# Causal attention: three fixed band buffers, blocks 2 and 0 of the queries in turns, fewer exponential and partial-sum buffers

## The chip, the cores and the metric

The kernel runs on one NeuronCore of a Trainium2 chip. A core has five engines that run side by side, each working through its own queue in order: TensorE (PE in the profile) multiplies matrices into eight PSUM banks, VectorE (DVE) reduces and adds, ScalarE (ACT) evaluates functions such as exp, GpSimd (POOL) does general arithmetic on SBUF, and SyncE (SP) issues DMA transfers. The metric is the device time of one execution in microseconds. The kernel before takes 4444.89 us, the median of 3 runs (4442.46 to 4447.12).

## The reference, cut to what matters

The whole is a chain of six residual layers on x of shape (2, 2048, 256): a mixture of experts, full attention, again the mixture, a gated recurrence, causal attention with relative positions, and the recurrence again. Only the fifth is changed:

```python
q = rotary(shape(x @ w_q.T)) / sqrt(16);  k = rotary(shape(x @ w_k.T));  v = shape(x @ w_v.T)
scores = einsum('bhqd,bhkd->bhqk', q, k)
rel = rel_emb[clip(pos_k - pos_q, -32, 32) + 32]
scores = scores + einsum('bhqd,qkd->bhqk', q, rel)
attn = softmax(where(causal, scores, -1e18))
ctx = einsum('bhqk,bhkd->bhqd', attn, v) + einsum('bhqk,qkd->bhqd', attn, rel)
out = ctx @ w_o.T
```

There are 16 heads of size 16. Because of the mask only relative positions from -32 to 0 occur, and all keys more than 31 behind a query share one position vector. Only a band of 32 keys behind each query therefore needs its own position terms.

## The kernel before, in words

The causal stage is `attention1`. Each batch's 2048 queries are cut into four blocks of 512 (`qc` 0 to 3), and the heads into four sets of four (`g`). A *group* is (batch, block, head set); there are 32. Block qc attends to the key blocks 0 to qc, so its size is 2(qc+1) *steps* of two half-steps each.

For each group there are two phases. In the score phase (`largest`), TensorE multiplies queries by keys and VectorE takes each query's largest score. The key vector shared by all far keys is folded into the keys (`kbias`), so far pieces need only a row maximum (L970). Near pieces, 160 keys wide, also get their own position term and their mask: they are added to a *band* tile in SBUF and written back to it (L986). The band comes from DRAM: `by_position` multiplies the queries by the position vectors (L924), ScalarE copies the product (L929), SyncE stores it skewed (L931) and reads it back shifted by one element per row (L939), which lines position terms up with keys. When a quarter of the band is done, the negated maximum is formed (L996) and added to the band on POOL (L1000); when all are done, SyncE stores the band to DRAM (pd, L1008).

In the exponential phase, TensorE computes the transposed far scores again (L1047, L1040) and brings the bands in by transposes (L1057, L1061), ScalarE takes exp into pT tiles (L1068), and TensorE multiplies these by the values half a step later (L1076). ScalarE copies each product to a `part` tile (L558) and POOL adds it to the output (L560). The position part of the output is read from pd (s<-pd, L1085), exponentiated (L1093), transposed (L1098) and multiplied (L1104). `divide` (L569 to L573) and `outputs` end a group.

Queries and keys are made by `rotate`: a projection (L138), a copy (L888), a shuffle (L890), and three or four POOL operations (L891 to L895); its temporaries, the product of `by_position` and the position exponentials share four `s2` buffers. Layer norms for the next blocks run on POOL too (L113).

The order on TensorE, ScalarE and VectorE is written out by hand. A loop over the groups fills Ms, Me (first and last score step), Es, Ee (exponential steps) and Rs (position step). Everything else is put at a step relative to these, and a last loop walks through the steps, interleaving the exponentials of one group with the scores of the next, head by head. The order on SyncE and POOL is made by a scheduler from dependencies. The groups of blocks 1 and 0 alternate, then come the four of block 2 and the four of block 3. Band tiles come from a pool of two buffers, so the plan lets a score phase start only when the band of the group two before it is nearly used up:

```python
if n > 1:
    start = max(start, min(Ee[n - 2] + 1, Es[n - 2] + 5) + 2 - (size - 2))
if n > 3:
    start = max(start, Ee[n - 4] + 4)
```

pT tiles have 12 buffers, part tiles 4.

Of the kernel before, what the change touches and what calls it, by code (L numbers as in the profile page):

```python
# [10 lines left out]
F32 = mybir.dt.float32  # L11
# [6 lines left out]
P = 128  # L18
B = 2
S = 2048  # L20
D = 256
H = 16
DH = 16
NT = B * S
NC = NT // P
TB = 512
NTB = NT // TB
CPB = TB // P
SB = S // TB
# [3 lines left out]
G = 4  # L33
J = 4
BAND = 32
BW = P + BAND
# [6 lines left out]
def macaron_kernel(ctx: ExitStack, tc: tile.TileContext, t: dict, out: bass.AP):  # L43
    nc = tc.nc
# [437 lines left out]
    HV = H // 2  # L482
    VW = DH + 1

    class Pieces:
# [32 lines left out]
        def values(self, v, wv, b, qc, half, row):  # L518

            w = HV * VW  # L520
            nc.gpsimd.memset(v[:, :, w:], 0.0)
            dst = v[:, :, 0:w].rearrange("p k (h d) -> p k h d", d=VW)
            nc.gpsimd.memset(dst[:, :, :, DH:], 1.0)
            pv = bank()
            for c in range(CPB):
                for kc in range(2):
                    nc.tensor.matmul(  # L527
                        pv[:, ts(c, P)], lhsT=self.xnT(b, qc)[:, kc, ts(c, P)],
                        rhs=wv[:, kc, ts(half, P)], start=kc == 0, stop=kc == 1,
                    )  # L530
            pv = pv.rearrange("p (k h d) -> p k h d", k=CPB, h=HV)
            if row is None:
                nc.scalar.copy(dst[:, :, :, 0:DH], pv)
            else:
                nc.vector.tensor_tensor(
                    dst[:, :, :, 0:DH], pv,
                    row[:, ts(half, P)].rearrange("p (o h d) -> p o h d", o=1, h=HV)
                    .to_broadcast([P, CPB, HV, DH]), ALU.add,
                )

# [7 lines left out]
                )  # L548
            nc.vector.tensor_tensor(self.q[t], self.q[t], pm, ALU.add)  # L549

        def gather(self, t, pv, q0=0):

            if t not in self.o:
                self.o[t] = self.wk.tile([P, TB], F32, name="o")
                nc.scalar.copy(self.o[t], pv)
                return
            part = self.wk.tile([P, TB], F32, name="part", bufs=4)
            nc.scalar.copy(part[:, q0:], pv[:, q0:])  # L558
            o = self.o[t][:, q0:]
            nc.gpsimd.tensor_tensor(o, o, part[:, q0:], ALU.add)  # L560
# [39 lines left out]
    class Jobs(dict):  # L600
        def at(self, step, fn, *args):
            self.setdefault(step, []).append((fn, args))
# [6 lines left out]
    def attention0(norm, tail, wq, wk_, wv, wo, bff):  # L609
# [7 lines left out]
        with ExitStack() as s:  # L617
            z = Pieces(s, "a0", norm, wo, bff)
# [50 lines left out]
            def weighted(t, kb):  # L669
                b, qc, g = groups[t]  # L670
                pv = bank()
                for j in range(J):
                    h = (g % 2) * J + j
                    nc.tensor.matmul(  # L674
                        pv[rows(j), :], lhsT=v[b, g // 2][:, kb, ds(h * VW, 32)],
                        rhs=z.pTs.pop((t, kb, j)), start=True, stop=True,
                    )
                z.gather(t, pv)

            jobs = Jobs()  # L680
            at = jobs.at
# [179 lines left out]
    def attention1(norm, tail, w, relk, relv, kbias, dramp, skew):  # L861
# [4 lines left out]
        with ExitStack() as s:  # L866
# [1 line left out]
            wk, q = z.wk, z.q  # L868
            groups = []
            for b in range(B):  # L870
                groups += [(b, qc, g) for g in range(G) for qc in (1, 0)]
                groups += [(b, qc, g) for qc in range(2, SB) for g in range(G)]
            NG = len(groups)
            kT, v, mx, band, cos, sin, wb, wT, st, pd, lead = ({} for _ in range(11))
            MX = SB + 1

            def tables(b, qc):
                for d, n in ((cos, "cos"), (sin, "sin")):
# [37 lines left out]
            def by_position(t):  # L916

                b, qc, g = groups[t]
                pr = bank()
                for qb in range(CPB):
                    nc.tensor.matmul(  # L924
                        pr[:, ts(qb, P)], lhsT=q[t][:, ts(qb, P)], rhs=relk,
                        start=True, stop=True,
                    )
                u = wk.tile([P, CPB * J, BAND], F32, name="s2", bufs=4)
                nc.scalar.copy(u.rearrange("p a d -> p (a d)"), pr)  # L929
                flat = skew[t % len(skew)]  # L930
                nc.sync.dma_start(  # L931
                    out=flat.rearrange("s (r w) -> r s w", w=UW)[:, :, P : P + BAND], in_=u
                )
                lead[t] = wk.tile([P, P - BAND + CPB * J * BW], F32, name="band")
                nc.gpsimd.memset(lead[t][:, 0 : P - BAND], 0.0)
                c = band[t] = lead[t][:, P - BAND :].rearrange(
                    "p (a j k) -> p a j k", a=CPB, j=J
                )
                nc.sync.dma_start(  # L939
                    out=c.rearrange("p a j k -> p (a j) k"),  # L940
                    in_=flat[:, P - 1 : P - 1 + P * (UW - 1)].rearrange(
                        "s (r w) -> r s w", w=UW - 1
                    )[:, :, 0:BW],
                )
# [119 lines left out]

            def exp(t, kb, j):
                q0 = max(0, kb - groups[t][1] * CPB) * P
                z.pTs[t, kb, j] = wk.tile([P, TB], F32, name="pT", bufs=12)
                nc.scalar.activation(z.pTs[t, kb, j][:, q0:], st.pop((t, kb, j))[:, q0:], AF.Exp)  # L1068

            def weighted(t, kb):  # L1070
                b, qc, g = groups[t]
                q0 = max(0, kb - qc * CPB) * P
                pv = bank()
                for j in range(J):
                    h = (g % 2) * J + j
                    nc.tensor.matmul(  # L1076
                        pv[rows(j), q0:],
                        lhsT=v[b, kb // CPB, g // 2][:, kb % CPB, ds(h * VW, 32)],
                        rhs=z.pTs.pop((t, kb, j))[:, q0:], start=True, stop=True,
                    )  # L1080
                z.gather(t, pv, q0)

            def positions_load(t):
                wb[t] = wk.tile([P, CPB, J * BAND], F32, name="s2", bufs=4)
# [17 lines left out]
            def positions(t):  # L1102
                pv = bank()
                nc.tensor.matmul(pv, lhsT=relv, rhs=wT[t], start=True, stop=True)  # L1104
                z.gather(t, pv)


            Ms, Me, Es, Ee, Rs = [], [], [], [], []
            for n, (b, qc, g) in enumerate(groups):
                size = 2 * (qc + 1)  # L1110
                start = Me[-1] + 1 if n else 0
                if n > 1:
                    start = max(start, min(Ee[n - 2] + 1, Es[n - 2] + 5) + 2 - (size - 2))
                if n > 3:
                    start = max(start, Ee[n - 4] + 4)
                Ms.append(start)
                Me.append(start + size - 1)
                start = Me[-1] + 2
                if n:
                    start = max(start, Ee[-1] + 1)  # L1120
                Es.append(start)
                Ee.append(start + size - 1)
                Rs.append(start + (3 if size == 2 else 4))
# [6 lines left out]
            jobs = Jobs()  # L1130
            at = jobs.at
            index = {x_: n for n, x_ in enumerate(groups)}
            for b in range(B):
                for qc in range(SB):
                    f = min(Ms[index[b, 1 if qc == 0 else qc, 0]], Ms[index[b, qc, 0]])
                    at(f - 12, tables, b, qc)
                    if b or qc > 1:
                        at(f - 12, z.ln_stats, b, qc)
                        at(f - 7, z.ln_transpose, b, qc)
                    for g in range(G):  # L1140
                        f = Ms[index[b, max(qc, 1), g]]
                        at(f - 4 + (qc == 0), keys, b, qc, g)
                    for half in range(2):
                        at(Es[index[b, max(qc, 1), 2 * half]] - 1 + (qc == 0), vals, b, qc, half)
            for n, (b, qc, g) in enumerate(groups):
                early = max(Ms[n] - 6, Ee[n - 4] + 1) if n > 3 else Ms[n] - 6
                at(early, queries, n)
                at(min(early + 2, Ms[n]), by_position, n)
                at(Me[n] + 1, z.subtract, n)
                at(Rs[n] - 3, positions_load, n)  # L1150
                at(Rs[n] - 2, positions_exp, n)
                at(Rs[n] - 1, positions_T, n)
                at(Rs[n], positions, n)
                end = max(Rs[n], Ee[n] + 1)
                at(end + 1, z.divide, n, b, qc, g, False)
                if g == G - 1:
                    at(end + 2, z.outputs_T, b, qc)
                    at(end + 3, z.outputs, b, qc, 0)
                    at(end + 4, z.outputs, b, qc, 1)
# [161 lines left out]
def _layout(i):  # L1321
# [47 lines left out]
        relv[d, a], relv0[d, a] = near, rel[0][None, :]  # L1369
        rel0[a, 0] = rel[0]  # L1370
    o["relk"], o["relk0"], o["relv"], o["relv0"], o["rel0_col"] = relk, relk0, relv, relv0, rel0
    o["a1_rel0_row"] = np.broadcast_to(np.tile(rel[0], H), (P, D))


    o["krow"] = np.zeros((P, 1), f)
# [29 lines left out]
```

## Time and profile before

| what | value |
|---|---|
| median of 3 runs | 4444.89 us (4442.46 to 4447.12) |
| profiled execution | 4446.38 us |
| its span, first to last instruction | 4444.6 us |
| mean granted TensorE clock | 0.969 |
| full attention stage, about | 440 to 2160 us |
| causal stage, first projection to last output | 2822 to 4259 us |
| instructions | 77325 |

The profile is of one execution. Times in its rows are microseconds from the span's start, durations of one instruction nanoseconds. PE is TensorE's multiplying, PEld its loading of weights. A matmul's end is modelled, so that TensorE's busy share overstates its work. A group is given by line, engine, operation and tiles (out<-in), then its count, busy time and mean, and the idle time of the engine before it with what ended that. A wait reads "who waited <- for what", with the total, the number and the longest. PEclk and the clock column are the share of full speed that TensorE was granted. A float32 matmul has two records, a transpose one.

### The profile page before, as it was taken

The page shows a single profiled execution, that of the slowest core. Times are in us where ns is not written, and L with a number is a line of the kernel's source. Part 1 is how long each engine was busy: PE and PEld are TensorE (multiplying, and loading weights), DVE is VectorE, ACT ScalarE, POOL GpSimd, SP SyncE. Part 2 cuts the span into 40 slices and gives each one's busy share as a digit, 9 for nine tenths or more (in the row PEclk, how much of TensorE's full clock was granted, in tenths as well). Part 3 has the DMA queues.
Part 4 walks back from the last instruction along what each step waited for, and adds up shares of the span by engine and source line. Part 5 has one row for each costly group of instructions (what it writes and reads, how often), then busy time and mean ns, then how long its engine had stood idle before and what let it go on. Part 6 is the DMA issues. An engine that isn't in the chain of part 4 may idle for free.

```text
span 4444.6 us, 77325 instructions
## 1 busy us (share of the span) xinstructions
PE 4178.2 (94%) x28512; PEld 2000.7 (45%) x28512; DVE 2711.3 (61%) x6176; ACT 2543.0 (57%) x5155; POOL 1825.1 (41%) x1694
## 2 busy tenths in 40 slices
PE   6798999999999999999968989799999999999999
PEld 3455433333343333333335545555544455554445
DVE  4234787887766778787442343455776645767633
ACT  2232488887877788888712322245566754566742
POOL 3226133335433333333350330366556576555520
PEclk8899999999999999999989999899999999999999
DMA  6242000000000000000232320254322344422201
GB/s 234 93 121 72 1 1 1 1 1 1 1 1 2 1 1 1 1 1 8 69 115 87 118 64 1 57 108 104 81 62 49 64 86 104 86 58 58 44 21 38
DMA packets 355514, 224.41 MB, mean 50 GB/s; under 512 B 146497, under 2 KB 338497, under 8 KB 355137
## 3 DMA queue, kind: packets, MB, share of 16 engines
q1 hardware_dynamic: 342848, 185.89, 16.7%
q0 software_dynamic: 12288, 33.57, 2.4%
q8 instruction: 227, 3.72, 0.4%
q14 instruction: 151, 1.23, 0.1%
HBM read 114.29 MB, written 105.12 MB: 49 GB/s over the span
## 4 chain that ended last, share of the span: by engine, by line
PE 82%; DVE 7%; POOL 3%; issue 3%; another core or an unknown queue 2%; DMA 2%; ACT 1%; SPq 0%; POOLq 0%; ACTq 0%; DVEq 0%
PE s L662 12%; PE s L674 11%; PE s L138 11%; PE s L650 10%; PE s L1076 5%; PE s L962 5%; PE s L358 5%; PE s L1047 5%; PE s L377 3%; PE s L592 1%; PE s L527 1%; PE s L1057 1%; PE s L1040 1%; PE s L1061 1%
## 5 line engine op out<-in xcount | busy, mean ns | idle before, releaser
L560 POOL TENSOR_TENSOR o<-o,part 128x512 f32<-128x512 f32 (+3 forms) x800 | 962.4, 1203 | 1418.9 <-ACT part L558 1414.6
L654 DVE TENSOR_REDUCE mx<-s 128x1 f32<-128x512 f32 x2048 | 1271.9, 684 | 365.4 <-PE s L650 364.4
L667 ACT ACTIVATE pT<-s 128x512 f32<-128x512 f32 x2048 | 1064.4, 618 | 207.3 <-PE s L650 202.4
L650 PE MATMUL s<-kT,q 32*128 32x512 f32 x4096 | 1016.6, 619 | 7.7 <-DVE mx L654 6.3
L662 PE MATMUL s<-q,kT 32*128 32x512 f32 x4096 | 1017.3, 617 | 6.3 <-DVE q L549 5.4
L1068 ACT ACTIVATE pT<-s 128x512 f32<-128x512 f32 (+3 forms) x1280 | 589.9, 546 | 269.6 <-PE s L1047 115.2
L662 PEld LDWEIGHTS s<-q,kT 32*128 32x128 f32 x4096 | 414.2, 184 | 472.2 <-DVE mx L654 310.5
L970 DVE TENSOR_REDUCE mx<-s 128x1 f32<-128x512 f32 (+1 forms) x768 | 472.0, 678 | 217.7 <-PE s L962 209.9
L558 ACT COPY part<-s 128x512 f32<-128x512 f32 (+3 forms) x800 | 466.6, 585 | 220.6 <-PE s L1076 101.9
L674 PE MATMUL s<-pT,v 128*32 128x512 f32 x4096 | 549.9, 605 | 2.0 <-DVE mx L654 1.9
L650 PEld LDWEIGHTS s<-kT,q 32*128 32x128 f32 x4096 | 405.4, 184 | 139.3 <-ACT pT L667 71.1
L358 PE MATMUL s<-we,xT 128*128 x592 | 289.1, 612 | 37.8 <-ACT xT L353 19.7
L962 PE MATMUL s<-kT,q 32*128 32x512 f32 (+7 forms) x2240 | 320.1, 437 | 2.8 <-ACT part L558 2.8
L1076 PE MATMUL s<-pT,v 128*32 128x512 f32 (+3 forms) x2560 | 306.6, 545 | 0.9 <-DVE mx L970 0.4
L365 DVE TENSOR_TENSOR h<-sg,s 128x256 f32<-128x256 f32 x148 | 62.1, 421 | 352.3 <-ACT sg L363 295.8
L403 POOL DMA_INDIRECT yg<-results,at x128 | 125.0, 977 | 314.9 <-PE s L358 104.9
L962 PE MATMUL s<-b,q 32*128 32x512 f32 (+7 forms) x1280 | 240.2, 528 | 5.7 <-POOL b L895 5.7
L674 PEld LDWEIGHTS s<-pT,v 128*32 128x32 f32 x4096 | 82.2, 108 | 338.2 <-ACT pT L667 282.6
L1047 PE MATMUL s<-q,kT 32*128 32x512 f32 (+3 forms) x1152 | 233.8, 516 | 0.0
L986 DVE CUSTOM_DVE_ANT_0 band<-s,band 128x160 f32<-128x160 f32 (+1 forms) x512 | 155.8, 314 | 82.9 <-PE s L1047 42.0
L1000 POOL TENSOR_TENSOR band<-band,mneg 128x640 f32<-128x640 f32 x128 | 160.9, 1260 | 94.0 <-DVE mneg L996 90.7
L1047 PE MATMUL s<-q,b 32*128 32x512 f32 (+3 forms) x896 | 195.6, 575 | 0.0
(208 smaller groups left out, 5549.1 us busy)
## 6 DMA issues: line engine op xcount, KB each, us to landing
band<-skew SPq DMA_DIRECT2D x32, 1280.0 KB
pd<-band SPq DMA_DIRECT2D x32, 1280.0 KB
xs<-places SPq DMA_DIRECT2D x148, 128.0 KB
results<-y SPq DMA_DIRECT2D x148, 128.0 KB
places<-zero SPq DMA_DIRECT2D x2, 4736.0 KB
we<-in_we SPq DMA_DIRECT2D x12, 768.0 KB
skew<-s SPq DMA_DIRECT2D x32, 256.0 KB
s<-pd SPq DMA_DIRECT2D x32, 256.0 KB
```

The source lines that it names most:

```text
L138: nc.tensor.matmul(ps, lhsT=w[:, kc, cols], rhs=rhs[:, kc, :], start=start and kc == 0, stop=stop and kc == 1,)
L358: nc.tensor.matmul(pu, lhsT=xT[i][:, ts(kc, P)], rhs=w[:, kc, ds(val[i], 2 * D)], start=kc == 0, stop=kc == 1,)
L560: nc.gpsimd.tensor_tensor(o, o, part[:, q0:], ALU.add)
L650: nc.tensor.matmul(ps, lhsT=q[t][rows(j), ts(qb, P)], rhs=kT[b, g][rows(j), ts(kc, TB)], start=True, stop=True,)
L654: nc.vector.tensor_reduce(mx[t][:, qb * J + j, kc : kc + 1], ps, AX.X, ALU.max)
L662: nc.tensor.matmul(st, lhsT=kT[b, g][rows(j), ts(kb, P)], rhs=q[t][rows(j), :], start=True, stop=True,)
L667: nc.scalar.activation(z.pTs[t, kb, j], st, AF.Exp)
L674: nc.tensor.matmul(pv[rows(j), :], lhsT=v[b, g // 2][:, kb, ds(h * VW, 32)], rhs=z.pTs.pop((t, kb, j)), start=True, stop=True,)
L962: nc.tensor.matmul(ps[:, ds(cols, n)], lhsT=lhsT, rhs=kT[b, c, g][rows(j), ds(k0, n)], start=True, stop=True,)
L1047: nc.tensor.matmul(ps[:, q0:], lhsT=k, rhs=q[t][rows(j), q0:], start=True, stop=True, skip_group_check=True,)
L1068: nc.scalar.activation(z.pTs[t, kb, j][:, q0:], st.pop((t, kb, j))[:, q0:], AF.Exp)
L1076: nc.tensor.matmul(pv[rows(j), q0:], lhsT=v[b, kb // CPB, g // 2][:, kb % CPB, ds(h * VW, 32)], rhs=z.pTs.pop((t, kb, j))[:, q0:], start=T ...
```

## The change

- The order of groups: per batch, four of block 1; then, per head set, block 2 and block 0; then four of block 3.
- Three band tiles are allocated for the whole stage and used in turn; their 96 leading zeros are written once.
- The plan waits for the exponentials of the group three before (`free`), and `by_position` stands at step `max(By, early + 1)`.
- pT tiles go from 12 buffers to 8, part tiles in this stage from 4 to 3. The row added to the values is 16 wide and broadcast over heads, instead of 256 wide.
- Queries are put down ahead of a step's other jobs; keys of blocks 0 and 1 go with the block-1 groups; the tables of cosines wait for the queries that used their buffers.

```diff
-                groups += [(b, qc, g) for g in range(G) for qc in (1, 0)]
-                groups += [(b, qc, g) for qc in range(2, SB) for g in range(G)]
+                groups += [(b, 1, g) for g in range(G)]
+                groups += [(b, qc, g) for g in range(G) for qc in (2, 0)]
+                groups += [(b, 3, g) for g in range(G)]
...
+            NBAND = 3
+            leads = []
+            for n in range(NBAND):
+                a_ = z.keep.tile([P, P - BAND + CPB * J * BW], F32, name=f"band{n}")
+                nc.gpsimd.memset(a_[:, 0 : P - BAND], 0.0)
+                leads.append(a_)
...
-                lead[t] = wk.tile([P, P - BAND + CPB * J * BW], F32, name="band")
-                nc.gpsimd.memset(lead[t][:, 0 : P - BAND], 0.0)
+                lead[t] = leads[t % NBAND]
...
-                z.pTs[t, kb, j] = wk.tile([P, TB], F32, name="pT", bufs=12)
+                z.pTs[t, kb, j] = wk.tile([P, TB], F32, name="pT", bufs=8)
...
-                z.gather(t, pv, q0)
+                z.gather(t, pv, 3, q0)
...
-                if n > 1:
-                    start = max(start, min(Ee[n - 2] + 1, Es[n - 2] + 5) + 2 - (size - 2))
+                free = Es[n - NBAND] + (4 if groups[n - NBAND][1] else 2) if n >= NBAND else -9
+                start = max(start, free + 4 - size)
                 if n > 3:
-                    start = max(start, Ee[n - 4] + 4)
+                    start = max(start, Ee[n - 4] + 2)
                 Ms.append(start)
                 Me.append(start + size - 1)
+                By.append(max(free, start - 3))
...
+            early = [
+                max(Ms[n] - 6, Ee[n - 4] + 1) if n > 3 else Ms[n] - 6 for n in range(NG)
+            ]
+            for n in range(NG):
+                at(early[n], queries, n)
             for b in range(B):
                 for qc in range(SB):
-                    f = min(Ms[index[b, 1 if qc == 0 else qc, 0]], Ms[index[b, qc, 0]])
-                    at(f - 12, tables, b, qc)
+                    f = Ms[index[b, max(qc, 1), 0]]
+
+                    done_ = {2: 1, 3: 0}.get(qc)
+                    free = early[index[b, done_, G - 1]] if done_ is not None else f - 12
+                    at(max(f - 12, free), tables, b, qc)
...
-                early = max(Ms[n] - 6, Ee[n - 4] + 1) if n > 3 else Ms[n] - 6
-                at(early, queries, n)
-                at(min(early + 2, Ms[n]), by_position, n)
+                at(max(By[n], early[n] + 1), by_position, n)
...
-    o["a1_rel0_row"] = np.broadcast_to(np.tile(rel[0], H), (P, D))
+    o["a1_rel0_row"] = np.broadcast_to(rel[0], (P, DH))
```

## The prediction

> **What bounds the kernel now.** I read the page first: TensorE's share, then its slices.
>
> ```profile
> PE 4178.2 (94%) x28512; PEld 2000.7 (45%) x28512; DVE 2711.3 (61%) x6176; ACT 2543.0 (57%) x5155; POOL 1825.1 (41%) x1694
> ...
> PE   6798999999999999999968989799999999999999
> ...
> PEclk8899999999999999999989999899999999999999
> ```
>
> TensorE looks full, in the causal stage (2822 to 4259 us) too. So I asked for busy times by stretch: four stretches in which groups of block 1 and block 0 alternate, then one group of block 2 and one of block 3.
>
> ```profile
> core 0: us, PE busy (x) PEld busy (x) DVE busy (x) ACT busy (x) POOL busy (x), PEclk, DMA share, GB/s
> 2903.30:2962.20 58.90, 54.53 (x489) 29.52 (x488) 32.60 (x128) 30.62 (x71) 40.20 (x38) 1.00 0.53 108
> 2962.20:3029.40 67.20, 61.71 (x521) 35.02 (x520) 36.06 (x138) 31.03 (x71) 47.60 (x46) 0.92 0.50 106
> 3601.80:3664.70 62.90, 57.65 (x500) 31.24 (x496) 33.40 (x129) 30.85 (x70) 40.05 (x37) 0.97 0.51 105
> 3664.70:3733.20 68.50, 61.90 (x524) 35.29 (x520) 36.06 (x138) 30.96 (x70) 46.34 (x44) 0.93 0.49 101
> 3176.60:3224.70 48.10, 48.00 (x427) 24.82 (x423) 32.34 (x90) 32.45 (x67) 30.61 (x28) 1.00 0.35 79
> 4085.20:4142.90 57.70, 57.52 (x498) 27.62 (x494) 41.45 (x105) 41.62 (x86) 32.55 (x29) 1.00 0.26 56
> ```
>
> The last two rows are full at full clock; the first four are not: 4 to 7 us idle each, the clock down to 0.92 in places. Why, the waits of SyncE's queue and the chain of waits say:
>
> ```profile
> SPq L1085 <- DMA pd<-band: 156.5, 19, 9.0
> SPq L939 <- PE s L1057: 144.4, 20, 15.4
> ```
>
> ```profile
> 2946.34 8.99 DMA s<-pd
> ...
> 3011.62 9.56 DMA s<-pd
> ...
> 3646.55 9.87 DMA s<-pd
> ...
> 3714.43 10.51 DMA s<-pd
> ```
>
> L939, the load of a band, waits until the transposes at L1057 have left one of two band buffers. And a load s<-pd stands on the chain once in each of the four stretches. ScalarE in the first:
>
> ```profile
> 2950.63 1.21 ACT L1068 ACTIVATE pT<-s 128x256 f32<-128x256 f32 x4 [0.42 <-PE s L1040]
> 2955.41 0.63 ACT L1093 ACTIVATE s<-s 128x512 f32<-128x512 f32 x1 [3.57 <-DMA s<-pd]
> ```
>
> Exponentials queue behind one that waits 3.57 us for that load, because SyncE issued it at 2946.34, after the next group's store pd<-band at 2945.88.
>
> **What the Trainium skill says.** "TensorE: Matmul & The Clock Gate", Part 1: idle of about one 3.4 us window halves the clock. Agrees: 0.92 and 0.93 in the stretches with gaps, 1.00 in the full ones. The table of the same page gives ScalarE, VectorE and GpSimdE strictly first-in first-out queues; the 3.57 us above shows it for ScalarE. "Perfetto Trace Analysis", Optimization Strategy: repeated equal bubbles can mean that there are too few buffers; the L939 waits are that. "Trainium Kernel Development and Optimization", Performance Expectations: matmul busy time is a bad measure of nearness to peak; here it counts 92% in stretches that, by the next part, lose 15%.
>
> **The change, step by step.**
>
> *The plan.* Worked out from the loop that fills Ms, Es: before, 193 steps, of which 127 have scores and exponentials, 33 scores alone, 33 exponentials alone. A block 1/block 0 pair takes nine steps, three of each kind, because the score steps of group n wait for the band of n-2. After, with three bands and pairs of blocks 2 and 0: 170 steps, 150 of both kinds, 10 and 10. The matmuls are the same ones, so I don't price a step; I price its columns.
>
> *TensorE's pace.* The records of the stage's matmuls (11,552) are as many as the code issues, so counting in program order gives each step its start. Content: columns at 0.838 ns (429 ns between starts of 512-column projections; 109 ns for 128-column transposes), a quarter of it for 32-row products, of which four run side by side. The 94 steps that pair blocks 2 and 3 took 730.4 us for 571.1 us of content: factor 1.28. Then:
> - the four stretches above: 257.5 us, content 171.7 x 1.28 = 219.7: 37.8 us to be had;
> - the two passages from pairs to block 2 (3029.4 to 3127.2, 3733.2 to 3831.1): 195.7 us, content 142.0 x 1.28 = 181.8: 13.9;
> - the start (2845.4 to 2903.3): 57.9 against 44.2; the first group has no exponentials beside it in either kernel, so I count 4 of 13.7;
> - the passage from batch 0 to 1 (3509.2 to 3601.8): 92.6 against 93.6: nothing, though it has steps of one kind.
> Sum 55.7 us.
>
> *Moved DMAs.* In the new order of SyncE's queue each block-1 load s<-pd stands ahead of the next group's pd store. For block 2, store and load still meet, but the load's exponential stands in the second half of the next step, some 12 us after the store, against 9.5 from store to landing above (2945.88 to 2955.41): the 3.57 us wait goes. This is within the 37.8. A band load is planned three steps ahead of its scores instead of four; block 0 needs it at once. Chain in the trace: copy 0.6, skew store until the band load's issue 6.1, band load 5.8 to 7.9 by its DMA records: 14.6 us at most, against three steps of about 7.5. Hidden by other groups' score and exponential steps; if that cover fell to two steps, nothing to a few us for each of eight groups. Tables of cosines wait for their buffers on the same queue, in both kernels; the skew store behind them has a step to spare.
>
> *Removed.* 32 memsets at L935, 178 ns: 5.7 us of POOL beside TensorE, nothing; three remain at the start. The rel row load shrinks from 128 to 8 KB under the recurrence; the addition at L535 keeps its 128x512 form (691 ns x 16).
>
> *pT from 12 to 8.* Eight are two half-steps. The matmuls that read the old ones are issued at the end of the half-step before the scores that the new exponentials need, on one in-order engine: nothing. Were that wrong, the wait would be about one matmul group, 1 us, in 320 half-steps.
>
> *part from 4 to 3.* ScalarE's copies may run three half-steps ahead of POOL, not four: 3.9 us less. Two layer norms in one step (POOL, at 3409) made four steps take 36.6 us where their like took 28.8; one layer norm in a block-2 step (3167) cost nothing. So 4 us more for the double, between 0 and 5 for each of four single ones; I take 0, upper end 20. The new one-kind steps at the passages to blocks 2 and 3: 3.
> Net: 55.7 - 7 = 48.7. Profiled execution 4446.4 - 48.7 = 4397.7; the median of the runs is 1.5 below that execution: **4396**.
>
> *POOL beside block 1.* The new bottleneck nearest by. One block-1 group now brings a query and two keys:
>
> ```profile
> L560 POOL TENSOR_TENSOR o<-o,part 128x512 f32<-128x512 f32 (+2 forms) x320 | 353.9, 1106 | 315.2 <-ACT part L558 312.0
> L1000 POOL TENSOR_TENSOR band<-band,mneg 128x640 f32<-128x640 f32 x128 | 160.9, 1260 | 94.0 <-DVE mneg L996 90.7 <-ACT part L558 2.7
> ...
> L894 POOL TENSOR_SCALAR s<-s,rel_col 128x512 f32<-128x512 f32 x32 | 50.2, 1568 | 1.9
> L891 POOL TENSOR_TENSOR q<-s,cos 128x512 f32<-128x512 f32 x32 | 40.8, 1275 | 49.7 <-ACT s L888 49.7
> ```
>
> Query 3 x 1.27, keys 2 x (3 x 1.27 + 1.57), bands 4 x 1.26, parts 8 x 1.11: 28.5 us, against about 34 of TensorE (content x 1.28). Before, 40 to 48 of 59 to 69.
>
> **Rivals.**
> *TensorE was nearer its bound than I say* (4430). Steps of near blocks carry many transposes: those with block 1 scores beside block 0 exponentials ran at 1.32 and block 0 beside 1 at 1.52. If the pairs and passages reach only 1.40 (content 313.7 x 0.12 = 37.6 us more), the gain is about 14. For: these are the steps that become common. Against: steps of block 2 scores beside 1 and 0 ran at 1.26 and 1.30, and the 1.52 steps hold the clock and DMA waits.
> *POOL decides* (4467, slower). POOL waits in order for ScalarE's copies before rotations, 2.05 us for each of 64 in the trace; three for a block-1 group make 34.6, TensorE's own pace. If these waits and the late part buffers push a group from 34 to 43 us, eight cost 72: 48.7 gained turn to 23 lost. It decides from 40 us a group. Against: few ScalarE waits fell on POOL before (9 us in the stage's part copies), and the queue has the slack of 5 us a group.
> *More is given back* (about 4370): the start's remaining 10 us, layer norms that no longer fall into pairs (two of those four stretches were 6 to 8 us longer than their fellows), and the clock at 1.00.
>
> **How the numbers follow.** Forecast 0.61, more given back 0.09, TensorE's bound 0.24, POOL 0.06. No change means within 0.2%, about 9 us, which a measurement of this kernel can just tell. Of the third, 4412 to 4440, 0.20 is faster by more and 0.04 within. Faster 0.90, same 0.04, slower 0.06. The likeliest case itself spans 4380 to 4410 (layer norms 0 to 20 us, the start 0 to 14). Low 4366 halves the second case, high 4430 takes two thirds of the third: 0.61 + 0.04 + 0.15 = 0.80.
>
> **What would show it.** Right: the stage some 50 us shorter and all else the same; the clock 0.99 or more beside block 1; no s<-pd in the chain for block-1 groups; SyncE's waits for L1057 well under 144 us. Wrong: POOL over 90% beside block 1 with ScalarE's part copies waiting for it; band scores (L986) waiting for DMA; VectorE's shuffles waiting for their buffers, as four s2 buffers serve more rotations per us; or the clock still near 0.92.

## The result, and the profile after

The changed kernel takes 4390.04 us, the median of 4 runs (4388.43 to 4390.93), against 4443.68 us for the kernel before (4 runs, 4436.19 to 4447.12). The ratio is 0.9881, with an interval from 0.9864 to 0.9898: 53.6 us less by the medians. The forecast was 4396 us, 48.7 us less.

The page of the changed kernel, its busy shares and two of its slices:

```profile
PE 4143.3 (94%) x28512; PEld 1982.5 (45%) x28512; DVE 2714.8 (62%) x6176; ACT 2545.9 (58%) x5155; POOL 1824.1 (42%) x1665
...
PE   6798999999999999999977989799999999999999
...
PEclk8899999999999999999988989999999999999999
```

It looks as full as before; a page like this can't show where 50 us went. The busy times by stretch can. In the view below the first row is ten steps in which block-1 groups stand beside each other; the next two rows are one pair of blocks 2 and 0 each, of batch 0, the two after them the like of batch 1, and the last is the whole causal stage. The columns are those of the prediction.

```profile
core 0: us, PE busy (x) PEld busy (x) DVE busy (x) ACT busy (x) POOL busy (x), PEclk, DMA share, GB/s
2875.70:2959.30 83.60, 83.10 (x805) 46.94 (x801) 52.55 (x190) 51.73 (x114) 56.76 (x49) 1.00 0.49 105
3019.80:3085.00 65.20, 64.67 (x595) 35.02 (x591) 44.03 (x146) 40.57 (x88) 38.64 (x35) 1.00 0.46 94
3085.00:3155.40 70.40, 66.52 (x600) 35.59 (x596) 45.02 (x151) 41.30 (x89) 45.55 (x42) 0.98 0.48 98
...
3745.10:3808.50 63.40, 62.52 (x584) 32.97 (x580) 44.07 (x151) 40.88 (x90) 38.18 (x36) 1.00 0.50 97
3808.50:3879.30 70.80, 67.11 (x609) 36.46 (x605) 43.03 (x144) 42.12 (x92) 45.95 (x42) 0.98 0.51 101
2813.70:4199.90 1386.20, 1335.27 (x11554) 696.05 (x11552) 894.66 (x2667) 848.42 (x1795) 840.61 (x755) 0.99 0.37 78
```

The stage before, in the same columns:

```profile
2822.60:4258.70 1436.10, 1365.75 (x11553) 714.04 (x11551) 890.54 (x2667) 845.77 (x1795) 844.52 (x784) 0.98 0.35 75
```

Beside block 1 TensorE now idles 0.5 us of 83.6, where it idled 4 to 7 us in each stretch of 59 to 69, and the clock is 1.00. The causal stage went from 1436.1 to 1386.2 us: 49.9 less. The two profiled spans differ by 57.9; the other 8.0 lie in stages whose code is the same. That rest took between 3000.5 and 3009.1 us in the thirteen profiles of this study, whatever the kernel, so the profiles compare stages well, and the kernels' times are compared by ratios over several runs. Two pairs, the stretches at 3085 and 3808, are still not full: about 4 us idle each at a clock of 0.98. They hold two of the layer norms and come back below.

The waits of SyncE's queue in the changed kernel:

```profile
SPq L946 <- DMA skew<-s: 93.6, 31, 7.9
SPq L1092 <- DMA pd<-band: 74.7, 9, 9.0
```

L946 is the band load. It waits now for its own skewed store, and 3 us in all for anything else; the wait for the transposes (144.4 us before) is gone. The wait of the load s<-pd for the store of pd is half of its 156.5 us, and no load s<-pd stands on the chain of waits any more. ScalarE waited for s<-pd 16.6 us in four places before, and waits 0.9 us once now. What the chain holds instead is this, its only rows of more than 2.5 us between the start and the end of the stage that are not TensorE's or maxima:

```profile
3131.95 4.84 POOL b L113 x4
...
3384.28 4.84 POOL b L113 x4
3391.79 4.85 POOL b L113 x4
...
3529.60 4.84 POOL b L113 x4
...
3806.03 4.84 POOL b L113 x4
```

L113 is the layer norm of a block of 512 tokens on POOL, four instructions of 1.22 us in one piece. The "double" layer norm is that of the second batch's first two blocks, which fall in one step. Before, only the double one was among the chain's long rows:

```profile
3422.49 4.83 POOL b L113 x4
3429.96 3.62 POOL b L113 x3
```

To see where each microsecond went, the prediction's own measure serves again: every step's time less 1.28 times its content; what is left is called the step's time *over pace*. The content of the stage is the same in all kernels (1348.8 us after the factor). The sum over pace was 87.3 us before and is 37.4 after:

| where | before | after |
|---|---|---|
| start (steps up to 8 before, up to 5 after; the latter holds one single layer norm) | 26.6 | 18.4 |
| the four stretches of blocks 1 and 0 | 37.9 | gone |
| the two passages to block 2 | 13.9 | gone |
| double layer norm, 3 to 5 steps | 7.8 | 9.0 |
| steps with one single layer norm (after: 38, 87 and 119) | within the stretches and the others | 5.3 + 4.1 + 5.0 |
| step 102: keys, query rotation and `divide` close together | none | 4.9 |
| steps of one kind or just after (22 and 138) | within the passages | 1.9 + 2.9 |
| end of the stage | 9.0 | 9.7 |
| all other steps | -7.9 | -23.8 |

### The profile page after: what moved, and what is told of

Same layout as the page of the kernel before. It is cut to its first block, busy times and chain, and to the rows that moved or that the text cites. A ratio compares the mean times of both kernels' runs of the same rounds, so it can differ in the third digit from the quotient of the medians.

```text
span 4386.7 us, 77337 instructions
## 1 busy us (share of the span) xinstructions
PE 4143.3 (94%) x28512; PEld 1982.5 (45%) x28512; DVE 2714.8 (62%) x6176; ACT 2545.9 (58%) x5155; POOL 1824.1 (42%) x1665
## 4 chain that ended last, share of the span: by engine, by line
PE 85%; DVE 5%; POOL 4%; issue 3%; another core or an unknown queue 1%; ACT 1%; DMA 1%; SPq 0%; POOLq 0%; ACTq 0%; DVEq 0%
PE s L662 13%; PE s L674 11%; PE s L138 11%; PE s L650 10%; PE s L1083 6%; PE s L358 6%; PE s L969 6%; PE s L1054 5%; PE s L377 3%; PE s L592 1%; PE s L1064 1%; PE s L527 1%; PE s L1047 1%; PE s L1068 1%
## 5 line engine op out<-in xcount | busy, mean ns | idle before, releaser
L969 PE MATMUL s<-kT,q 32*128 32x512 f32 (+7 forms) x2240 | 333.3, 436 | 4.9 <-ACT part L558 4.6
L1054 PE MATMUL s<-q,b 32*128 32x512 f32 (+3 forms) x896 | 210.7, 568 | 0.0
```

The costliest lines, as they stand in the source:

```text
L969: nc.tensor.matmul(ps[:, ds(cols, n)], lhsT=lhsT, rhs=kT[b, c, g][rows(j), ds(k0, n)], start=True, stop=True,)
L1054: nc.tensor.matmul(ps[:, q0:], lhsT=k, rhs=q[t][rows(j), q0:], start=True, stop=True, skip_group_check=True,)
```

## The experiments

Three theories stood at the start. *Order and bands*: the change gains because score steps find a free band, so that fewer steps hold one kind of work alone. *Load order*: it gains because the loads s<-pd no longer block ScalarE's queue. *Layer norms*: it leaves a part on the table, because layer norms in one piece delay what is behind them on POOL. All ratios are to the kernel before, run on the same chip in the same session; medians are named where they help.

**The old order of groups with the new bands.** In the changed kernel, two lines:

```diff
-                groups += [(b, 1, g) for g in range(G)]
-                groups += [(b, qc, g) for g in range(G) for qc in (2, 0)]
-                groups += [(b, 3, g) for g in range(G)]
+                groups += [(b, qc, g) for g in range(G) for qc in (1, 0)]
+                groups += [(b, qc, g) for qc in range(2, SB) for g in range(G)]
```

> The changed kernel with the old order of groups (blocks 1 and 0 alternate, then 2, then 3); three bands, eight pT, three parts stay. Its plan has 177 steps, 143 of both kinds, 17 and 17. Mine (packing the phases is the gain, about 2.4 us for each step that the plan loses, 55.7 us for 23): 7 steps fewer packed than the changed kernel's 170, so 17 us more, 4400 to 4415. Rival, the third band alone is the gain: within 5 us of the changed kernel, 4385 to 4395. Rival, the new order alone is the gain: back near the kernel before, 4435 to 4450.

Measured: 4427.66 us, ratio 0.9976 (0.9966 to 0.9987). All of the change but its order brings a fifth of the gain, less than I expected. Its chain of waits says why, with three pieces that are not in the changed kernel's:

```profile
2911.53 12.35 DMA band<-skew
3035.22 12.29 DMA band<-skew
3732.37 12.43 DMA band<-skew
```

Steps 11, 24 and 110, the first score step of a block-0 group each time, took 10.4, 12.4 and 12.6 us over their pace. The plan lets a block-0 group begin two steps after its band is free, and these three loads took longer than that: each was issued 0.4 us behind another group's store of pd. Three other block-0 groups have the same two steps and no such store ahead of their loads; they are at most 0.5 us over pace.

**The same with one step more of cover for block 0.** On top of the old order:

```diff
-                start = max(start, free + 4 - size)
+                start = max(start, free + (3 if size == 2 else 4 - size))
```

> The changed kernel with the old order of groups again, but the plan starts a block-0 score phase three steps after its band buffer is free instead of two. Plan: 181 steps, 139 of both kinds, 21 and 21. Theory that late band loads decide (in the run with the old order three of them stood on the chain with 12.3 us each): faster than that run by 25 to 35 us, ratio to before 0.989 to 0.993, though it has four steps more. Theory that the number of packed steps decides: slower than that run by 4 x 2.4 = 10 us, ratio 0.999 to 1.001.

Measured: 4408.46 us, ratio 0.9911 (0.9895 to 0.9928). The plan is longer, 181 steps against 177, and the kernel is faster by 0.65%. The waits of VectorE for the band load, of the old order and then of this kernel:

```profile
DVE band L992 <- DMA band<-skew: 43.1, 5, 12.6
```

```profile
DVE band L992 <- DMA band<-skew: 17.9, 3, 7.5
```

So a count of steps doesn't price a plan, and the 2.4 us per step that I had put into the expectations was wrong. A step of one kind costs little when TensorE is fed in it; what costs is a step whose data are late. Loads issued behind a store of pd are still on its chain (13.4 us at 3038, 14.0 us at 3722), but with one step more no first score step of a block-0 group is over 2.0 us over pace. Even so the old order still waits more than the new one, which puts six steps of block-2 scores between two block-0 groups (10.4 us, shown further down).

**Two bands in the new order.**

```diff
-            NBAND = 3
+            NBAND = 2
```

The plan follows from the number: bands come free a group later, and every band load of a block-0 group is planned two steps ahead of its scores. In the changed kernel that is so in batch 1 only; in batch 0 there are three steps.

> The changed kernel with two band buffers in its plan and memory; the new order stays. Its plan has 179 steps, 141 of both kinds, 19 and 19. Mine: 9 steps more, 22 us, plus what the bands of block-0 groups come late by, since they are now ordered only two steps ahead of their scores: 4405 to 4425. Rival, the order alone is the gain: 4385 to 4395. Rival, the third band is everything: 4435 to 4450.

Measured: 4471.71 us, ratio 1.0081 (1.0064 to 1.0097): slower than the kernel before, and outside all three ranges. Waits and chain of this kernel:

```profile
DVE band L993 <- DMA band<-skew: 139.0, 16, 15.3
POOL band L990 <- DMA band<-skew: 82.4, 8, 14.3
```

```profile
2938.25 7.79 DMA pd<-band
...
2946.52 4.03 DMA skew<-s
2950.57 7.12 DMA band<-skew
...
3019.80 13.68 DMA band<-skew
...
3105.36 6.72 DMA band<-skew
...
3175.58 11.67 DMA band<-skew
```

At 2938 the store of pd, the skewed store and the band load stand one after the other: the load s<-pd waits at the head of SyncE's queue for the store of pd to land, and the skewed store, whose copy began at 2944.6, was issued only 0.4 us after that landing. At 3019.8 the band load was issued 0.4 us after another group's store of pd (3019.4), and took 13.7 us. The first score steps of the eight block-0 groups were 14.3, 9.5, 15.0, 9.2, 13.0, 9.5, 15.2 and 11.2 us over their pace, 97 us together. They take turns between two kinds. In the longer four the band load was issued 0.4 to 1.4 us behind another group's store of pd and took 11.7 to 13.7 us. In the other four it took 6.4 to 6.7 us, but stood in SyncE's queue behind a load s<-pd that waited 5.0 to 5.5 us for its store. The new order without the third band is slower than the kernel before; the two parts belong together.

**How much cover the band load needs.** Cover is the number of steps from the planned `by_position` to the scores. With three bands, two steps instead of three:

```diff
-                By.append(max(free, start - 3))
+                By.append(max(free, start - 2))
```

> The changed kernel with the position products, and with them the band's way through DRAM, two steps ahead of the scores instead of three. My prediction had it at nothing to a few us for each of eight block-0 groups: up to 25 us more than the changed kernel, ratio to before at most 0.994. After the run with two bands (9 to 15 us in each such group): 5 to 10 us each, 40 to 80 us more, ratio 0.997 to 1.006.

Measured: 4396.14 us, ratio 0.9904 (0.9887 to 0.992), the stage 4.2 us longer than the changed kernel's. The intervals of the two ratios overlap. VectorE's waits for the band load, of this kernel and then of the changed one:

```profile
DVE band L993 <- DMA band<-skew: 12.6, 5, 3.8
```

```profile
DVE band L993 <- DMA band<-skew: 10.4, 4, 4.0
```

The edit reaches less than I meant: in batch 1 `free` already leaves a block-0 group two steps in the changed kernel, so only the four of batch 0 lost one. Their first score steps changed by 3.0, 0.0, -2.4 (a step with a layer norm) and 1.2 us, and the first of these loads, 6.1 us at 3009, is on the chain. In batch 1 of the changed kernel the two steps left 0.7, 0.2 and 0.2 us over pace, beside the 5.0 of a layer norm step. This falls where the prediction put it ("nothing to a few us for each of eight groups"). It also shows what was wrong with two bands. There from the skewed store to the issue of the band load it took 4.5 to 7.3 us, and from there to the first finished quarter 7.5 to 14.8; here mostly 3.0 and 7 to 11. So the lost step of cover is not what made those late; the stores and loads of other groups, as told above, are.

**Fewer buffers alone.** In the kernel before, pT from 12 to 8 and part from 4 to 3 in this stage:

```diff
-                z.pTs[t, kb, j] = wk.tile([P, TB], F32, name="pT", bufs=12)
+                z.pTs[t, kb, j] = wk.tile([P, TB], F32, name="pT", bufs=8)
...
-                z.gather(t, pv, q0)
+                z.gather(t, pv, q0, 3)
...
-                z.gather(t, pv)
+                z.gather(t, pv, 0, 3)
```

> The kernel before with eight pT and three part buffers in the causal stage, nothing else. Mine: nothing for pT, 4 us for the double layer norm, up to 5 for each single one: 4440 to 4460, within 0.3% of before. Rival, buffers are what holds the changed kernel back: 4460 or more.

Measured: 4441.27 us, ratio 1.0012 (1.0005 to 1.0019), 4 to 5 us slower than its own before. As expected, and in the place expected: the steps of the double layer norm (77 to 81) went from 7.8 to 13.5 us over their pace, and nothing else grew by more than 1.5 us. In the one profile other steps came out shorter by as much (two by 2.4 us), so that the stage there is no longer than before; the loss rests on the runs' times. The smaller pools by themselves don't make single layer norms costlier in the old plan.

**The position part one step later.** In the kernel before, without the change:

```diff
-                at(Rs[n] - 2, positions_exp, n)
-                at(Rs[n] - 1, positions_T, n)
-                at(Rs[n], positions, n)
-                end = max(Rs[n], Ee[n] + 1)
+                at(Rs[n] - 1, positions_exp, n)
+                at(Rs[n], positions_T, n)
+                at(Rs[n] + 1, positions, n)
+                end = max(Rs[n] + 1, Ee[n] + 1)
```

> The kernel before with the position part of each group (exponential, transposes, product) one step later; its load stays where it was. Mine (ScalarE's wait for s<-pd in block-1 groups delays the steps with the transposes, 17.5 us in five of them): 10 to 18 us faster than before, ratio 0.996 to 0.998. Rival (the band buffers' wait hides it): ratio 0.999 to 1.001.

Measured: 4417.75 us, ratio 0.9935 (0.9919 to 0.9952): 29 us by the medians, more than I gave it, with the stage 25 us shorter. No s<-pd is on its chain. The four stretches lost 17.1 of their 37.9 us over pace, the passages 2.2, the double layer norm 3.9, and the rest is spread. The surprise is in SyncE's waits of this kernel:

```profile
SPq L939 <- PE s L1057: 169.1, 20, 14.9
SPq L1085 <- DMA pd<-band: 134.5, 16, 8.9
```

The wait for a band buffer did not shrink; it grew from 144.4 to 169.1 us. The prediction had read its two SyncE rows together. This run takes one apart from the other: a queue may stand still for 169 us and cost little by that, while an exponential that is placed too early behind a 9 us load costs more than its wait of 16.6 us. I put the surplus down to ScalarE's other exponentials and the weighted products that queue behind it; it wasn't measured apart, and the edit moves the transposes and the product of the position part too. About half of the gain could be had without bands or order.

**Layer norms moved to VectorE.** In the changed kernel:

```diff
-            self.norm.normal(blk, nc.gpsimd)
+            self.norm.normal(blk, nc.gpsimd if self.bias is not None else nc.vector)
```

> The changed kernel with the layer norms of the causal stage applied on VectorE instead of POOL. Steps that follow a layer norm took 4 to 10 us more than their content in the changed kernel's trace, some 30 us in all. Mine (POOL is blocked by the layer norm, ScalarE's part copies then wait for POOL): 4360 to 4375. Rival (it is the transposes or VectorE's own statistics that are late): within 5 us of the changed kernel, 4385 to 4395.

Measured: 4409.91 us, ratio 0.9942 (0.9926 to 0.9959), slower than the changed kernel by 0.6%; every expectation missed. VectorE's wait in front of L113 (23.6 us and six of the nine times are the moved instructions; the rest is the next stage's layer norms, on VectorE in every kernel):

```profile
DVE b L113 <- POOL rstd L102: 29.6, 9, 5.3
```

The root of the variance is still made on POOL, and VectorE stands up to 5.3 us before it with the maxima and mask additions of the scores behind. The Trainium skill, "Perfetto Trace Analysis", in a note under Tensor Engine Instruction, says that ScalarE, VectorE and GpSimd execute strictly first in, first out; the 23.6 us agree for VectorE. The steps after a layer norm shrank (38 from 5.3 to 0.7 us over pace) and the steps before them grew by more (37 from 0.1 to 6.8). The lump was moved, not removed, and to the engine that feeds the scores.

**Layer norms cut up.** In the changed kernel, statistics of one quarter per step, the root a step of its own, and two quarters of the normalization in each of two steps, still on POOL:

```diff
-                        at(f - 12, z.ln_stats, b, qc)
+                        for c in range(CPB):
+                            at(f - 13 + c, norm.stat, b * SB + qc, c)
+                        at(f - 10, norm.root, b * SB + qc)
+                        for c in range(CPB):
+                            at(f - 9 + c // 2, ln_piece, b * SB + qc, c)
```

`ln_piece` holds one of the four instructions of L113.

> The changed kernel with each causal layer norm cut up: statistics of one chunk a step, the root, then two chunks a step on POOL, the same instructions in all. Mine (a layer norm in one piece holds POOL for 6 us or more and ScalarE's part copies wait behind it, 29 us after six layer norms in the changed kernel's trace): 12 to 25 us faster than the changed kernel, ratio to before 0.982 to 0.986. Rival (the sum of POOL's work decides, not its lumps): as the changed kernel, 0.987 to 0.990.

Measured: 4367.17 us, ratio 0.9823 (0.9807 to 0.984), about 26 us below the changed kernel by the ratios; the stage is 26.7 us shorter. What ScalarE's copies to `part` wait for POOL, changed kernel first, then this one:

```profile
ACT part L558 <- POOL o L560: 13.7, 7, 4.6
```

```profile
ACT part L558 <- POOL o L560: 3.9, 4, 2.3
```

Step 38 went from 5.3 to 0.3 us over pace, 69 to 71 from 9.0 to 0.4, 87 from 4.1 to -0.3, 119 from 5.0 to 0.8, step 5 from 6.0 to 3.4. The chain's rows of L113 on POOL are gone. How one lump of 6 us on POOL reaches TensorE, the changed kernel's timeline of POOL at step 38 shows (start, duration, what):

```profile
3130.48 0.24 POOL L100 TENSOR_SCALAR ve<-mv 128x4 f32<-128x4 f32 x1
3130.80 1.04 POOL L102 TENSOR_TENSOR rstd<-ve,mhalf 128x4 f32<-128x4 f32 x1
3131.95 4.84 POOL L113 TENSOR_SCALAR b<-x,mv,rstd 128x256 f32<-128x256 f32 x4
3136.76 1.26 POOL L1007 TENSOR_TENSOR band<-band,mneg 128x640 f32<-128x640 f32 x1
...
3140.43 1.26 POOL L560 TENSOR_TENSOR o<-o,part 128x512 f32<-128x512 f32 x1
```

For 6.3 us POOL adds nothing to any output and no band. `divide` at L569 needs the finished sum; TensorE stood idle for it for 3.2 us from 3138.5. In the steps 70, 87 and 119 it is ScalarE that finds all three part buffers full.

The cut spreads the statistics on VectorE as well, eight instructions that took 2.1 us in one piece. In the steps above the chain runs through the POOL rows and not through the statistics. In step 5 it is the other way round: the chain holds the statistics and no POOL row, and POOL was done with the layer norm before its next input came:

```profile
2864.26 4.84 POOL L113 TENSOR_SCALAR b<-x,mv,rstd 128x256 f32<-128x256 f32 x4
2870.73 1.31 POOL L899 TENSOR_TENSOR b<-s,cos 128x512 f32<-128x512 f32 x1 [1.63 <-ACT s L896]
```

So of the 6.0 us of step 5 only the 2.6 that went with the cut are the layer norm's, and not by way of POOL.

**The same with the next batch's first layer norm four steps earlier.**

```diff
+                        f0 = f - (4 if b and qc == 0 else 0)
```

and f0 in place of f in the lines above and for the transpose that follows.

> As the run with the layer norms cut up, and that of the second batch's block 0 stands four steps ahead of that of its block 1, so that no two fall together. Mine: 3 to 7 us more than without this. Rival: nothing more, within 3 us.

Measured: 4368.81 us, ratio 0.9824 (0.9808 to 0.9841): no difference from the run above. After the cut, two layer norms side by side cost nothing more, so there was nothing to gain; expectation missed.

**Layer norms cut and positions late, in the kernel before.** Both edits above, without the change:

> The kernel before with its two bands and its old order, with the position part one step later and the layer norms cut up. Steps after a layer norm took about 20 us over their content in the kernel before. If the three bands and the new order carry a gain of their own beside the position wait: 15 to 20 us below the run with the later position part, 4400, ratio to before 0.989 to 0.991, and still 25 to 35 us above the changed kernel with layer norms cut up (0.9823). If the change's gain was the position wait alone: within 8 us of that kernel, ratio 0.981 to 0.984.

Measured: 4412.56 us, ratio 0.994 (0.9923 to 0.9956), the same as with positions late alone (0.9935). The stage is 6.0 us shorter, which the ratios can't tell: the double layer norm went from 3.9 to 0.3 us over pace, and steps 23 and 117, each after a single one, from 1.7 and 3.3 to 0.5. So the old plan hides most of its layer norms, not all. Set beside the cut in the changed kernel (0.9823) this also gives what the rest of the change is worth when neither late position loads nor layer norms in one piece are in play: 0.0117 of 4440 us, 52 us. That rest is bands and order together with the new places of queries, keys and tables; the latter were not tried alone.

**The best version.** The cut, and the keys of block 2 one step earlier, away from the query rotations of step 102:

```diff
-                        at(f - 4 + (qc == 0), keys, b, qc, g)
+                        at(f - 4 + (qc == 0) - (qc == 2), keys, b, qc, g)
```

> The changed kernel with the layer norms cut up and the keys of block 2 one step earlier. If the wait of the divisions for POOL in the step after keys and a query (4.6 us once in the changed kernel) goes: 2 to 5 us faster than without, ratio 0.981 to 0.982. Otherwise the same, 0.982 to 0.983.

Measured: 4363.6 us, ratio 0.9831 (0.9814 to 0.9847). Step 102 went from 4.6 us over pace to -0.1 and the stage from 1359.5 to 1352.9 us, but by the ratios it can't be told from the cut alone. Both beat the changed kernel; of the 37.4 us over pace 4.1 are left, and the largest terms are the start (16.4, counted as in the table) and the end (9.2) of the stage.

## Why the prediction was right, and where it was not

The time came out 6 us below the forecast and inside the range, and the gain is where the prediction put it: 49.9 us in the causal stage. That the sum came so near is in good part luck; its parts held as follows.

**Four stretches and two passages.** All of the 37.8 and 13.9 us came, to within the measure: no such stretch is left, and what new steps lose is counted below. The two rows of SyncE from which they were argued are not of equal worth, though. The late position loads are worth 25 us of the stage in the kernel before, by the run with the position part one step later; the band buffers' waiting can stand at 169.1 us in a kernel that is faster. The Trainium skill, "Perfetto Trace Analysis", Optimization Strategy, which the prediction names for these waits, speaks of gaps on the engine that should be saturated; that is TensorE here, and the 144.4 us were SyncE's. With both edits of the last experiment but one in place, the rest of the change brings 52 us more than the old plan, so the second half of the argument carries a gain of its own too. That it comes from scores and exponentials standing side by side fits TensorE's 0.5 us of idle time beside block 1, but it wasn't varied alone, and a count of such steps did not foretell the old order's time. The shares overlap, since in the new plan the position loads are early as well.

**The pace of 1.28.** Block-1 steps beside each other ran at 1.29 of their content, block 2 beside 1 at 1.31, block 2 beside 0 at 1.26, blocks 2 and 2 at 1.24. The rival of 1.40 is refuted for these. Block 0 beside 0 ran at 1.55 and block 0 beside 2 at 1.36, but those few steps hold only 75 us of content and two of the layer norms. All other steps ran a little better than 1.28, 16 us in sum over the change. Why is open.

**Layer norms: the step that failed.** "One layer norm in a block-2 step (3167) cost nothing. So 4 us more for the double, between 0 and 5 for each of four single ones; I take 0, upper end 20." Measured: 1.2 us more for the double, and 5.3, 4.1 and 5.0 us for three of the four single ones (steps 38, 87, 119), 14.4 us; the fourth, in step 5, is worth 2.6. That is near the upper end. Cutting them all gave the time back, 26 us. The row at 3167 was of a plan with slack around it; I carried its zero to a plan in which I had just taken the slack away. It was not a fair sample of the old plan either: steps 23 and 117, after two other single layer norms, were 5.1 and 5.4 us over pace there, of which the later positions took 3.4 and 2.2, and the cut 1.2 and 2.8 more. Fewer part buffers are not enough as a cause: they cost the old plan about 5 us, and only the double one grew. Whether a fourth buffer would hide the lumps in the new plan was not tried.

**The start.** I gave it 4 us of the 13.7 that stood from the first score step on. That part shrank by 3.0, with the layer norm of step 5 in it; the steps before the first scores, of which I had said nothing, went from 13.0 to 7.8. Why is open.

**The sum.** Gains: stretches and passages 51.8, start 8.2, other steps 15.9. Losses: double layer norm 1.2, three single ones outside the start 14.4, step 102 4.9, steps of one kind 4.8 (3 predicted), end 0.7. Net 49.9, against 48.7 predicted with 55.7 less 7. The total was right by luck: two errors of about 20 us, a gain too small and a loss too small, took each other away. The rival "more is given back", 4370, was what the kernel would have reached with its layer norms cut (4367.17 us).

**Moved DMAs.** The band load is three steps ahead of block-0 scores only in batch 0, and two in batch 1; the prediction's "three steps" overlooked `free`. Both were enough: VectorE waited 10.4 us for band loads in the whole stage, and two steps throughout cost 4.2 us of it. What I did not see is that the cover needed depends on what else is in flight: with two bands the same load held VectorE up to 15.3 us. pT at 8 cost nothing that shows.

**POOL as the bound.** POOL was busy 56.8 of 83.6 us beside block 1, 68%, or 22.7 us for each group's four steps where my sum had 28.5, and no group stretched. The rival erred in the amount and was right in the engine: a POOL busy 65% of the stretches at 3085 and 3808 set the end of a step where one piece of 6 us stood before an addition that TensorE or ScalarE waited for.

**The clock.** The prediction says that the trace agrees with the idle window of about 3.4 us. It agrees only in direction. By the profile TensorE's longest single gap was 1.8 and 2.4 us in the stretches at 0.92 and 0.93, and the first stretch stood at 1.00 with gaps of up to 1.6 us. What lowered the clock there is open.

## What to carry to other kernels

When an edit takes slack out of a schedule, price again every long piece that the slack had been hiding; a piece that cost nothing before is no evidence for after. Try cutting long side work on an in-order engine into pieces of a microsecond or two at their own steps before moving it to another engine. A queue's long wait has no price of its own: look for who is late by it, and test the cheapest edit that removes the lateness, here a job placed one step later, before the large one.

## What the runs showed that I had not expected

- A 6 us piece on POOL, 0.1% of the program, took 4 to 5 us from TensorE in three places of the new plan, and no time at 3167 in the old one; moving it to VectorE, where the instruction takes 0.48 us on average instead of 1.22, lost 0.6% instead.
- A band load took 6.0 to 7.2 us on the chain of the two-band kernel, and 11.7 to 13.7 us the four times that it was issued 0.4 to 1.4 us behind another group's store of pd. The late loads of the old order (12.3 to 12.4 us) were of the same kind.
- Placing the position part one step later, which took ScalarE's wait for s<-pd from 16.6 to 1.0 us, gained 25 us of the stage.
- The stages that no edit touched varied by 8.6 us from one profile to the next (3000.5 to 3009.1), as much as some effects that were looked for.
